# A macaron transformer block on one core: the second expert layer's scatters in eight pairs, each in a piece of its own

## The chip, the core and the metric

The kernel runs on one core of a Trainium2 chip. A core has five engines with queues of their own: PE (TensorE, matrix products), ACT (ScalarE, activation functions), DVE (VectorE, elementwise work and reductions), POOL (GpSimd, here mostly the issue of indirect DMAs) and SP (SyncE, plain DMAs). The time is the device time of one execution in microseconds (us); less is better.

## The reference

The input is one sequence of 4096 tokens with 256 features, in float32. Three residual steps follow each other:

```
x = x + 0.5 * ffn(layernorm(x))
x = x + attention(layernorm(x))        # 16 heads of 16
x = x + 0.5 * ffn(layernorm(x))        # the same weights as the first

ffn(x):  scores = softmax(x @ Wg)                  # 32 experts
         weights, indices = top_k(scores, 4)
         for e in 32 experts:
             tok = tokens that chose e              # at most 2048
             y[tok] += swiglu(x[tok], W1[e], W2[e], W3[e]) * w[tok]
         return y + swiglu(x, Ws1, Ws2, Ws3)        # a shared expert of width 256
swiglu = silu(x @ w1) * (x @ w3) @ w2
```

So each expert layer has to bring every token's row to four experts, and the attention lies between the two layers.

## The kernel before

The program has seven stages in order: `first_front` (normalizing, routing and the shared expert of layer 0), `Layer.experts` of layer 0, `projections` (queries, keys, values), `attention`, a tail inside `attention` (lines 1394 to 1440), `Layer.experts` of layer 1, and a last loop that adds up and stores.

**Routing** is `Layer.route` (lines 204 to 363), a Python generator. Every `yield` ends a *piece*: whoever drives the generator decides where in the program the next piece is placed. For a block of tokens it normalizes (L140 to L172), transposes on PE (L180), computes the gate (L233), takes the four largest scores (L254, L255), counts positions with two products (L276), works out slots (L293 to L342), and at its end sends rows: for each of its token tiles and each of the four choices POOL issues one indirect DMA (L353) which writes 128 rows of 264 floats to the slots named in `sidx`. In layer 0 a chunk has eight tiles (32 scatters), in layer 1 a block has four (16 scatters). The scatters declare no dependency on each other. `sidx`, an integer tile for the whole layer, is written by one DVE addition (L345); L346 and L347 then make the weights `wk`. All 16 scatters of a block lie in one piece.

**The attention loop** walks over 1024 steps: 8 blocks of 512 queries, 4 groups of 4 heads, 32 key tiles. In a step PE makes the scores of four heads two steps ahead (L1257), ACT takes exponentials (L1267) from PSUM banks in a ring, and PE multiplies them with the values (L1275). At a group's end DVE divides (L1295 to L1311). Hooks placed with `at(n, f)` run behind step n's value products: query loads (L1378), the addition of a shift to the queries (L1379), block loads (`load_x`, L1246 to L1248, called from L1381), the output projection of a finished block (`project_out`, L1353 and L1361), and the pieces of that block's way into layer 1. These last come from `front` (L1327): the pieces of `layer.route`, then for blocks 0, 1 and 2 those of `layer.shared` (the shared expert, L378 to L411), for blocks 3, 4 and 5 two stores; the shared expert of blocks 3 to 7 is done in the tail. `front` hands out `PIECES` = 24 calls, which are placed at every third step, in steps 3 to 24 of each group of the following block; there are 28 such places:

```
free = [
    m
    for m in range(n + 9, n + 1 + NG * NT)
    if 3 <= (m - n - 1) % NT <= 24 and (m - n - 1) % 3 == 0
]
for m, f in zip(free, front(b)):
    at(m, f)
```

A routed block needs ten pieces, so its scatters stand in the tenth, at step 45 of the following block. Blocks 0 to 6 are routed in the loop, block 7 in the tail.

**Order.** PE, ACT, DVE and SP keep the program's order (`manual_schedule` with ORDERED, L57); each engine works through its queue in order. A block's tokens lie in a tile `xq` of which there are two, so `load_x(nb)` can start once block nb - 2 is done with; it is called at step 2 of the last group of block nb - 1. Pieces that need a PSUM bank borrow the accumulator that is not in use (`Banks.tile`), and the steps beside them do with the ring alone.

**Tail.** After the last step, the shared expert of the blocks put off is interleaved with the route of block 7 by `next(route)`, and `share_out` prepares the extra blocks of the experts. `Layer.experts` then reads the scattered rows expert by expert.

Of the kernel before, what the change touches and what calls it, by code (L numbers as in the profile page):

```python
# [10 lines left out]
I32 = mybir.dt.int32  # L11
U32 = mybir.dt.uint32
AF = mybir.ActivationFunctionType
ALU = mybir.AluOpType
# [4 lines left out]
P = 128  # L19
# [14 lines left out]
QT = QB // P  # L34
# [6 lines left out]
K = 4  # L41
# [8 lines left out]
NSLOT = E * S0 + NOVMAX * BO  # L50
CLEARED = E * S0 + NOV * BO
LATER = (3, 4, 5, 6)
PIECES = 24
RW = D + 2 * K
KR = K + 1
BIG = float(1 << 20)
# [4 lines left out]
def kernel(  # L61
# [14 lines left out]
    nc = tc.nc  # L76
# [109 lines left out]
    class Layer:  # L186
# [17 lines left out]
        def route(self, ch, xt, pool, pm):  # L204
# [3 lines left out]
            n, t0 = self.n, ch * self.n  # L208
            count, held, total, shift = self.count, self.held, self.total, self.shift
            chunk = slice(t0, t0 + n)  # L210
            shape = [P, n, E]

            def tile(shape, name, dtype=F32, bufs=1):
                return pool.tile(shape, dtype, tag=name, name=name, bufs=bufs)
# [36 lines left out]
            top = tile([P, n, 8], "top")  # L251
# [87 lines left out]
            slot = tile([P, n, K], "slot")  # L339
# [2 lines left out]
                nc.vector.tensor_reduce(slot[:, :, k], hot[k][:], AX.X, ALU.add)  # L342
            beyond = tile([P, n, K], "beyond")
            nc.vector.tensor_scalar(beyond[:], slot[:], BIG, -BIG, ALU.is_ge, ALU.mult)
            nc.vector.tensor_add(self.sidx[:, chunk, :], slot[:], beyond[:])  # L345
            nc.vector.tensor_scalar(beyond[:], slot[:], BIG, 0.5, ALU.is_lt, ALU.mult)  # L346
            nc.vector.tensor_mul(self.wk[:, chunk, :], top[:, :, 0:K], beyond[:])  # L347


            group = f"scatter{self.index}"  # L350
            for t in range(n):
                for k in range(K):
                    ins = nc.gpsimd.indirect_dma_start(  # L353
                        out=self.xg[:],
                        out_offset=bass.IndirectOffsetOnAxis(
                            ap=self.sidx[:, t0 + t, k : k + 1], axis=0
                        ),
                        in_=xr[:, t, :],
                        in_offset=None,
                    ).ins  # L360
                    tc.declare_no_dep(ins, group=group, reason="rows of their own")
                    tc.add_to_no_dep_group(group, ins)
            yield

        def shared(self, ch, xt, xT, pool, pm):
# [801 lines left out]
    class Banks:  # L1167
# [18 lines left out]
        def tile(self, shape, dtype, tag, name):  # L1186

            self.lent = 1
            if self.over:
                self.next = (self.next + 1) % (self.RING + 2)  # L1190
            bank = self.all[:, self.next if self.over else self.other(), :]
            n = 1
            for m in shape[1:]:
                n *= m
            names = "abcd"[: len(shape) - 1]
            sizes = dict(zip(names, shape[1:]))
            return bank[:, :n].rearrange(f"p ({' '.join(names)}) -> p {' '.join(names)}", **sizes)
# [20 lines left out]
    def attention(layer, kT, v, shift, keep):  # L1218
# [5 lines left out]
        with (  # L1224
# [12 lines left out]
            def load_queries(b, g):  # L1237
                q = q_tiles[(b * NG + g) % 3]
                read_queries(q, b, g)
                qs[b, g] = q  # L1240

            def shift_queries(b, g):
                q = qs[b, g]
                nc.vector.tensor_scalar(q[:], q[:], shift[:], None, ALU.add)

            def load_x(b):  # L1246
                xs[b] = pool.tile([P, QT, D], F32, tag="x", name="xq")
                nc.sync.dma_start(xs[b][:], x1_at[:, b * QT : (b + 1) * QT, :])  # L1248
# [75 lines left out]
            def at(n, f):  # L1324
                later.setdefault(n, []).append(f)

            def front(b):  # L1327
# [18 lines left out]

                return [piece] * PIECES

# [26 lines left out]
            for n, (b, g, t) in enumerate(steps):  # L1375
                if t == 0 and n + NT < len(steps):
                    nb, ng, _ = steps[n + NT]
                    at(n + 2, lambda nb=nb, ng=ng: load_queries(nb, ng))  # L1378
                    at(n + 11, lambda nb=nb, ng=ng: shift_queries(nb, ng))  # L1379
                    if ng == 0:  # L1380
                        at(n + 2, lambda nb=nb: load_x(nb))  # L1381

            ahead = 2
# [15 lines left out]
            def half(b, xt, xT):  # L1399
                halves[b] = layer.shared_half(xt, xT, b * QT, pool, pm, bufs=2)  # L1400

            half(last - 1, xs[last - 1][:], layer.xT)
            for b in LATER[:-1]:
                both = pool.tile([P, HG, QB], F32, tag="ex", name="ex", bufs=3)
                n = NC * QB
# [6 lines left out]
            def go_on(b, pieces=1):  # L1412
                for _ in range(pieces):
                    next(halves[b])

            go_on(last - 1, 2)
            for i in range(0, QT, 2):
                project_out(last, i)
            route = layer.route(last, xs[last], pool, pm)
            next(route)  # L1420
            next(route)
            go_on(last - 1)
            go_on(LATER[0])
            for _ in range(NC + 1):
                next(route)
# [2 lines left out]
            for _ in range(3):  # L1428
                next(route)
            go_on(LATER[0])  # L1430
            for _ in range(2):
                next(route)
            half(last, xs[last][:], layer.xT)
            rest = [*LATER[1:-1], last]
            go_on(rest[0])
# [53 lines left out]
    with tc.tile_pool(name="keep0", bufs=1) as keep:  # L1489
        layer = Layer(0, keep, 2 * QT, nc.scalar.copy)  # L1490
        low = first_front(layer, keep)
        layer.experts(low)

        side = ctx.enter_context(tc.tile_pool(name="side", bufs=1, side="right"))
        with tc.tile_pool(name="kv", bufs=1, side="right", reuse_waits="tile") as kv:
            kT = kv.tile([P, NG, T], F32, name="kT")
            v = kv.tile([P, NT, NH, HV], F32, name="v")
            shift, flag = projections(layer, (side, kT, v))
            large = nc.values_load(flag[0:1, 0:1], min_val=0, max_val=1)
            with tc.If(large > 0):  # L1500
                take_maxima(kT)
            layer = Layer(1, side, QT, nc.vector.tensor_copy)
            attention(layer, kT, v, shift, side)
# [76 lines left out]
```

## Time and profile before

| what | value |
|---|---|
| median of 3 runs | 3525.7 us (3518.18 to 3526.12) |
| the profiled execution | 3541.41 us |
| its span, first to last instruction | 3539.7 us |
| PE busy | 3096.2 us (87%) |
| ACT busy | 2318.5 us (66%) |
| DVE busy | 954.2 us (27%) |
| POOL busy | 614.1 us (17%) |
| attention loop, first to last value product | 795 to 3091 us of the span |
| tail, then experts of layer 1 | from 3089 us and from some 3175 us |
| granted PE clock, mean | 0.934 |

The profile's page gives busy time by engine and by groups of instructions. A group's line names the source line, the engine, the operation and the tiles (out<-in), the count, then busy time and the mean of one in ns, then the engine's idle time ahead of it and what ended most of that. "issue" and "remote" stand for a wait whose releaser the profile does not show. The chain of work is the path followed back from the last instruction: start, length, what. A window row gives, for a stretch of time, the busy time and number of instructions of each engine, the granted PE clock as a share of full speed, and the DMA engines' share.

### The profile page before, as it was taken

Reading aid. Unit: us, or ns where it says so; the run is one execution under the profiler, and the core shown is the slowest. Engines: PE = TensorE matmul, PEld = TensorE weight load, DVE = VectorE, ACT = ScalarE, POOL = GpSimd, SP = SyncE. Lnnn points to the kernel's source line nnn. Section 1 sums busy time; section 2 is a strip of 40 time slices with the busy share of each in tenths; the row PEclk is TensorE's granted clock in tenths of the full one; section 3 lists DMA queues with packets and bytes.
Section 4 is the critical chain, followed back from the end, with each engine's and each line's share of the span. In section 5 each row is a group of like instructions: output and inputs, shape, how many; then the busy total and the mean of one; then the engine's idle time right before and its main releaser. Section 6 shows DMA issues by size and latency. Waiting matters only on the chain.

```text
span 3539.7 us, 50151 instructions
## 1 busy us (share of the span) xinstructions
PE 3096.2 (87%) x20043; PEld 1061.2 (30%) x20043; DVE 954.2 (27%) x2804; ACT 2318.5 (66%) x3732; POOL 614.1 (17%) x647
## 2 busy tenths in 40 slices
PE   5547886979999899899999989989989999979890
PEld 3224554432222222222222212212222221246550
DVE  5442334740002202211210210211121120154337
ACT  2101221449998799799889889989979988912220
POOL 3354654110000100100100010010010010025551
PEclk7678998989999999999999999999999999989995
DMA  6125665844110000000000000000000000036657
GB/s 239 69 87 191 223 216 175 238 128 141 57 38 3 25 16 3 27 16 3 23 19 3 16 33 3 15 33 4 9 33 10 3 18 10 21 121 226 222 194 302
DMA packets 141795, 284.07 MB, mean 80 GB/s; under 512 B 32480, under 2 KB 83296, under 8 KB 141152
## 3 DMA queue, kind: packets, MB, share of 16 engines
q1 hardware_dynamic: 90960, 176.85, 15.2%
q0 software_dynamic: 31872, 97.56, 7.7%
q10 hardware_dynamic: 18704, 6.20, 0.7%
q8 instruction: 163, 2.67, 0.3%
q14 instruction: 96, 0.79, 0.1%
HBM read 145.07 MB, written 131.27 MB: 78 GB/s over the span
## 4 chain that ended last, share of the span: by engine, by line
PE 71%; issue 3%; DVE 2%; DMA 1%; ACT 0%; another core or an unknown queue 0%; POOL 0%; SPq 0%; DVEq 0%; POOLq 0%; ACTq 0%
PE banks L1257 32%; PE banks L1275 29%; PE h L723 4%; PE o L745 2%; DVE xt L770 1%; PE xbt_ps L697 1%; PE banks L424 1%; PE banks L1353 1%; PE banks L378 1%; PE banks L446 0%; PE banks L233 0%; PE banks L398 0%; ACT ex L1267 0%; PE banks L180 0%
## 5 line engine op out<-in xcount | busy, mean ns | idle before, releaser
L1267 ACT ACTIVATE ex<-banks 128x512 f32<-128x512 f32 (+1 forms) x3224 | 2058.7, 714 | 230.8 <-PE banks L1257 110.6
L1257 PE MATMUL banks<-q,kT 32*128 32x512 f32 x8192 | 1188.6, 646 | 81.3 <-issue 42.8
L1275 PE MATMUL banks<-ex,v 128*17 128x512 f32 x8192 | 1085.5, 602 | 0.0
L353 POOL DMA_INDIRECT xg<-xr,sidx x256 | 246.5, 963 | 2413.5 <-DVE beyond L346 2226.9
L1257 PEld LDWEIGHTS banks<-q,kT 32*128 32x128 f32 x8192 | 330.8, 185 | 931.8 <-ACT ex L1267 746.6
L1295 DVE COPY o<-banks 128x512 f32<-128x512 f32 x32 | 22.1, 692 | 1403.4 <-ACT ex L1267 771.9
L1275 PEld LDWEIGHTS banks<-ex,v 128*17 128x17 f32 x8192 | 136.3, 95 | 785.2 <-issue 784.2
L753 POOL DMA_INDIRECT ys<-yb,toi x304 | 292.4, 962 | 218.9 <-DVE yb L751 83.3
L723 PE MATMUL h<-xT,w 128*128 128x512 f32 x512 | 251.3, 637 | 0.0
L732 ACT ACTIVATE s<-h 128x512 f32<-128x512 f32 (+1 forms) x112 | 51.7, 461 | 171.1 <-PE h L723 107.8
L703 ACT COPY xT<-xbt_ps 128x512 f32<-128x512 f32 (+1 forms) x112 | 50.6, 451 | 171.3 <-PE o L745 68.2
L745 PE MATMUL o<-w,hT 128*128 128x256 f32 x512 | 127.0, 389 | 18.9 <-issue 17.0
L723 PEld LDWEIGHTS h<-xT,w 128*128 128x128 f32 x512 | 101.5, 209 | 105.2 <-issue 105.2
L749 ACT COPY yb<-o 128x512 f32<-128x512 f32 x64 | 37.5, 586 | 118.6 <-PE o L745 81.1
L734 DVE TENSOR_TENSOR hT<-s,h 128x512 f32<-128x512 f32 (+1 forms) x112 | 57.8, 516 | 198.7 <-PE h L723 69.4
L1298 DVE RECIPROCAL den<-den 128x512 f32<-128x512 f32 x32 | 107.3, 3353 | 1.1
L745 PEld LDWEIGHTS o<-w,hT 128*128 128x128 f32 x512 | 93.6, 192 | 42.7 <-issue 29.0
L697 PE MATMUL xbt_ps<-ident,xb 128*128 128x128 f32 x512 | 74.1, 290 | 26.5 <-DMA xb<-xg 17.5
L770 DVE SCALAR_TENSOR_TENSOR xt<-y,wk,xt 128x256 f32<-128x256 f32 x192 | 93.1, 485 | 6.9
L701 DVE COPY xT<-xbt_ps 128x512 f32<-128x512 f32 (+1 forms) x112 | 57.9, 517 | 127.4 <-PE xbt_ps L697 86.9
L433 ACT ACTIVATE th<-sh_ps 128x512 f32<-128x512 f32 x16 | 9.2, 596 | 123.5 <-remote 70.5
L446 PE MATMUL so<-ws_sb,shT 128*128 128x256 f32 x128 | 47.4, 509 | 45.8 <-issue 23.7
(245 smaller groups left out, 1826.8 us busy)
## 6 DMA issues: line engine op xcount, KB each, us to landing
y<-ys SPq DMA_DIRECT2D x64, 640.0 KB
xb<-xg SPq DMA_DIRECT2D x62, 528.0 KB
w<-in_wexp_dram SPq DMA_DIRECT2D x64, 384.0 KB
xg<-zeros SPq DMA_DIRECT2D x152, 132.0 KB
xg<-zero SPq DMA_DIRECT2D x32, 264.0 KB
xbb<-xg SPq DMA_DIRECT2D x48, 132.0 KB
ys<-yb,toi POOLq DMA_INDIRECT x304
q<-qd SPq DMA_DIRECT2D x128, 34.0 KB
```

What stands on the lines that cost most here:

```text
L353: ins = nc.gpsimd.indirect_dma_start(out=self.xg[:], out_offset=bass.IndirectOffsetOnAxis(ap=self.sidx[:, t0 + t, k : k + 1], axis=0), in_ ...
L697: nc.tensor.transpose(tp[:, i * P : (i + 1) * P], xb[:, i, c * P : (c + 1) * P], ident[:])
L701: nc.vector.tensor_copy(xT[:, c, : n * P], tp[:, : n * P])
L723: nc.tensor.matmul(ps[:, : n * P], w[:, (j * NC + c) * H : (j * NC + c + 1) * H], xT[:, c, : n * P], start=(c == 0), stop=(c == NC - 1),)
L734: nc.vector.tensor_mul(hT[:, : n * P], s1[:, : n * P], h[1][:, : n * P])
L745: nc.tensor.matmul(o[:, i, :], hT[:, (i0 + i) * P : (i0 + i + 1) * P], w2, start=True, stop=True)
L753: ins = nc.gpsimd.indirect_dma_start(out=ys[:], out_offset=bass.IndirectOffsetOnAxis(ap=b["toi"][:, i : i + 1], axis=0), in_=yb[:, i, :], ...
L770: nc.vector.scalar_tensor_tensor(xt, y[:, k, :], self.wk[:, t, k : k + 1], y[:, K, :] if k == 0 else xt, ALU.mult, ALU.add,)
L1257: nc.tensor.matmul(pm.all[:, banks[j], :], kT[rows, g, t * P : (t + 1) * P], q[rows, :], start=True, stop=True,)
L1267: nc.scalar.activation(ex[:, i : i + n, :], pm.all[:, k : k + n, :], AF.Exp, scale=SCALE)
L1275: nc.tensor.matmul(acc[j * HP : j * HP + HV, :], v[:, t, g * HG + j, :], ex[:, j, :], start=(t == 0), stop=(t == NT - 1),)
L1298: nc.vector.reciprocal(den[:], den[:])
```

## The change

In layer 1 a block's 16 scatters are no longer in one piece: they go in eight pairs, and after each pair the generator yields, so each stands in a piece of its own, three steps behind the one before it. The final slots are left in the float tile `slot`, and ahead of each pair DVE copies the pair's two columns into a small integer tile `to` (16 of these), which the scatters of the pair use. In layer 0 the scatters stay together; there the addition that writes `sidx` moves behind the making of `wk`, in both layers `kept` is a tile of its own beside `beyond`. A routed block now has 18 pieces in place of ten, so `PIECES` grows to 28. `load_x(nb)` moves from the last group of block nb - 1 to step 2 of block nb itself. In the tail, the rest of the route is run to its end in place of two calls of `next`, so that the order there is as before apart from the copies.

```diff
-PIECES = 24
+PIECES = 28
...
             beyond = tile([P, n, K], "beyond")
             nc.vector.tensor_scalar(beyond[:], slot[:], BIG, -BIG, ALU.is_ge, ALU.mult)
-            nc.vector.tensor_add(self.sidx[:, chunk, :], slot[:], beyond[:])
-            nc.vector.tensor_scalar(beyond[:], slot[:], BIG, 0.5, ALU.is_lt, ALU.mult)
-            nc.vector.tensor_mul(self.wk[:, chunk, :], top[:, :, 0:K], beyond[:])
+            kept = tile([P, n, K], "kept")
+            nc.vector.tensor_scalar(kept[:], slot[:], BIG, 0.5, ALU.is_lt, ALU.mult)
+            nc.vector.tensor_mul(self.wk[:, chunk, :], top[:, :, 0:K], kept[:])
+            if self.index == 0:
+                nc.vector.tensor_add(self.sidx[:, chunk, :], slot[:], beyond[:])
+            else:
+                nc.vector.tensor_add(slot[:], slot[:], beyond[:])
...
             group = f"scatter{self.index}"
+
+            m = K if self.index == 0 else 2
             for t in range(n):
+                to = self.sidx[:, t0 + t, :]
                 for k in range(K):
+                    if self.index > 0 and k % m == 0:
+                        to = pool.tile([P, K], I32, tag="to", name="to", bufs=4 * QT)
+                        nc.vector.tensor_copy(to[:, k : k + m], slot[:, t, k : k + m])
                     ins = nc.gpsimd.indirect_dma_start(
                         out=self.xg[:],
-                        out_offset=bass.IndirectOffsetOnAxis(
-                            ap=self.sidx[:, t0 + t, k : k + 1], axis=0
-                        ),
+                        out_offset=bass.IndirectOffsetOnAxis(ap=to[:, k : k + 1], axis=0),
                         in_=xr[:, t, :],
                         in_offset=None,
                     ).ins
...
+                    if self.index > 0 and k % m == m - 1:
+                        yield
             yield
...
-                    if ng == 0:
+                    if ng == 1 and nb > 0:
                         at(n + 2, lambda nb=nb: load_x(nb))
...
-            for _ in range(2):
-                next(route)
+            for _ in route:
+                pass
             half(last, xs[last][:], layer.xT)
```

## The prediction

> **What bounds the kernel now.** I read the page's groups first, for who does the work and what the scatters cost their own engine.
>
> ```profile
> L1267 ACT ACTIVATE ex<-banks 128x512 f32<-128x512 f32 (+1 forms) x3224 | 2058.7, 714 | 230.8 <-PE banks L1257 110.6
> L1257 PE MATMUL banks<-q,kT 32*128 32x512 f32 x8192 | 1188.6, 646 | 81.3 <-issue 42.8
> ...
> L353 POOL DMA_INDIRECT xg<-xr,sidx x256 | 246.5, 963 | 2413.5 <-DVE beyond L346 2226.9
> ```
>
> The attention loop (795 to 3091 us) is two thirds of the span, and ACT and PE keep each other busy there: ACT's exponentials alone take 2058.7 of its 2296 us, and PE makes a step in 2.054 us. POOL is idle nearly throughout, so its 963 ns per scatter cost nothing as POOL time. The line to stop at is PE's 42.8 us of "issue": PE waits, and nothing visible lets it go.
>
> Then the chain of waits, in the stretch of the loop around one block's 16 scatters (POOL issues them from 2334.54 to 2354.4):
>
> ```profile
> 2340.16 0.98 PE banks L1275 x8
> 2341.14 1.29 issue
> 2342.43 1.14 PE banks L1257 x8
> 2343.57 0.98 PE banks L1275 x8
> 2344.56 8.51 issue
> 2353.06 2.09 PE banks L1257 x8
> 2355.15 2.20 PE banks L1275 x8
> ```
>
> Away from the burst the chain has 1.07 and 0.98 us for the two products of a step. Here PE loses 1.29 and 8.51 us, then runs at about half speed (2.09 and 2.20), and is back at 1.07 only from 2364.70 on. The same engine order, seen from ACT in the timeline:
>
> ```profile
> 2327.91 12.21 ACT L1267 ACTIVATE ex<-banks 128x512 f32<-128x512 f32 x18
> ...
> 2343.17 0.60 ACT L1267 ACTIVATE ex<-banks 128x512 f32<-128x512 f32 x1 [0.79 <-remote]
> ...
> 2352.41 0.60 ACT L1267 ACTIVATE ex<-banks 128x512 f32<-128x512 f32 x1 [6.75 <-remote]
> ```
>
> ACT's wait of 6.75 us ends first, PE's 8.51 us end at 2353.06, as soon as that exponential has freed its bank. All matmuls that ACT could be waiting for were over at 2344.6. So during a long run of scatters the engines stop getting work from each other. PE gaps of over 1 us inside the loop occur at the seven bursts and nowhere else.
>
> To price it I cut windows from one score product to another, each with exactly 13 steps, 104 instructions of L1257 (columns: window, length, PE busy, weight loads, granted clock, DMA share, GB/s). The first three are blocks with the shared expert, the next four without, the last is undisturbed.
>
> ```profile
> 1158.13:1204.45 46.32, 16.89 (x104) 4.67 (x104) 0.85 0.13 48
> 1454.87:1499.83 44.96, 15.18 (x104) 4.26 (x104) 0.89 0.14 49
> 1750.34:1795.69 45.35, 15.07 (x104) 4.26 (x104) 0.92 0.13 48
> 2046.12:2088.13 42.01, 16.50 (x104) 4.47 (x104) 0.88 0.14 52
> 2332.80:2374.85 42.05, 16.50 (x104) 4.47 (x104) 0.88 0.14 52
> 2619.52:2660.27 40.75, 15.99 (x104) 4.46 (x104) 0.87 0.15 54
> 2904.95:2947.90 42.95, 17.38 (x104) 4.67 (x104) 0.80 0.14 51
> 1000.00:1026.70 26.70, 14.82 (x104) 4.06 (x104) 1.00 0.15 53
> ```
>
> The seven sum to 304.39 us, seven undisturbed ones to 186.90: 117.5 us more. Each of the first three also holds three pieces of the shared expert, which the chain shows at 1.91 us apiece away from any burst (at 1190.47): 9 x 1.91 = 17.2. What is left, 100.3 us or 14.3 per burst, is the price of the bursts, clock loss included (0.80 to 0.92 in place of 1.00). DMA bandwidth isn't it: the undisturbed window has the same 53 GB/s, from clearing stores.
>
> **What the change does, part by part.**
>
> *The burst becomes eight pairs.* Pieces stand three steps apart, 3 x 2.054 = 6.2 us (more across a group's end). A pair takes POOL 2 x 0.96 + 0.30 = 2.2 us, so POOL rests about 4 us between pairs. What does a pair cost the loop? In the timeline ACT runs without a gap until 2340.12, 5.6 us after the first scatter, which is five scatters; in the burst of 1159.9 until 1167.5, 7.6 us. The experts' stage shows the recovery: its run of ten POOL issues from 3207.15 to 3219.5 has one PE gap of 1.16 us late in it, the run of twelve to 3237.2 ends in one of 2.89 us, the run of six from 3241.49 has none, with POOL pauses of only 2.3 to 4.3 us between. So the nearest row puts a pair at 0. The other bound is proportion, 100.3 / 112 = 0.9 us per scatter, under which pairs gain nothing. I take 0, because the first five scatters of a burst are the same operation in the same place. Gain: 100.3 us.
>
> *A rule against it.* The Trainium skill, "SBUF — State Buffer", section "Who interferes with whom", says that DMA never contends with a compute engine and that PE and ACT never wait on anyone. By the rule the bursts don't hold ACT, their spacing gains 0, and the sum would be 3528 us. The rows above show ACT and PE standing still in every long run of scatters. Measurement decides, and I use the row. It can't be an artefact of profiling either: the profiled execution took 3541.4 us, the median of the plain runs 3525.7, and those 15.7 us leave no room for 100.
>
> *Eight DVE copies per block.* The nearest row is the 128x1 COPY of L307, 0.147 us: 8 x 0.147 = 1.2 us. In the loop DVE is busy 5.93 of 100 us (window 2400 to 2500), so this hides; a query shift or a division queued behind a copy starts 0.15 us later, with steps to spare. In the tail it is not hidden: at 3138.76 PE has waited 9.54 us for DVE's u (L439), which stands behind the route, so all eight copies come ahead of it: +1.2 us (0 to 2). The tail's 16 scatters still follow each other, so its own stall stays.
>
> *POOL's new waits.* Each pair waits for its copy. Only the next pair is queued behind it on POOL, and its rows are read after the tail, some 200 us later at the closest: 0.
>
> *Layer 0.* The first scatter of each of four chunks now waits for two more DVE operations of 0.18 us (rows of L344 and L346): 0 to 1.6 us, I take 1.0 as three of the four bursts sit in a stretch where everything waits for them.
>
> *Pieces and borrowed banks.* The eight new pieces use no PSUM bank. The six shared pieces per block move eight places back and keep their 1.91 us each; 25 pieces fit the 28 places.
>
> *load_x.* It moves past 32 steps of SP's queue. Its buffer was given up by a store that stands ahead of it in that queue, and its first reader, the output projection, comes over 120 steps (250 us) later: 0. Were that cover gone, a 512 KB load at the page's best 302 GB/s would cost an estimated 1.7 us per block, 12 in all.
>
> Sum against the profiled execution: 3541.4 - 100.3 + 1.2 + 1.0 = 3443.3 us. Against the median, 15.7 lower: **3427.6, forecast 3428**.
>
> **Rivals.** *(B) A rest stays with each pair.* The smallest late release seen is ACT's 0.79 us above. 56 pairs x 0.79 = 44 us: 3472. For it: in these steps ACT has no slack. Against it: none of the first five scatters of any burst shows one. *(C) The stall goes by number.* If it came after so many scatters whatever their pace, two per block of half the length would give the same sum: about 3528. Against it: the experts' stage issues hundreds of indirect DMAs in runs of 6 to 18 and shows no wait of that size except late in a run. *(D) Slower.* Every pair makes ACT and PE miss one step, because a start of POOL from rest disturbs them (the first scatter of the burst at 1159.9 took 1.20 us in place of 0.96). Price 2.05 us, place the 56 pair pieces, 115 us against 100 saved: 3428 + 115 = 3543. It decides from 1.8 us per pair (100.3 / 56). Against it: burst starts show no missed step.
>
> **How the numbers follow.** A 0.76, B 0.13, C 0.03, D 0.08. A's own spread: the plain runs may stall 10% less than the profiled one (gain 90), the tail and layer 0 may cost 0 to 4; with the spread of the runs (8 us) that is 3415 to 3442. To leave out no more than two in ten the range goes up into B, to 3465. About 0.3% (10.6 us) is what a measurement of this kernel can tell from no change. Faster by more: A and B, 0.89; within: C, 0.03; slower: D, 0.08.
>
> **What would show it.** Right: windows of 13 steps around the pairs take 26.7 us plus 1.91 per shared piece, clock 1.00; "issue" on L1257 falls from 42.8 to a few us; ACT's "remote" waits vanish from the loop; 56 pairs of scatters some 6.2 us apart; the tail's PE wait on L439 is about 1 us longer. Wrong: gaps of ACT right behind each pair (B or D), or one long wait at about the fourth pair (C). The forecast falls if what holds ACT is not how long POOL issues without a rest.

## The result, and the profile after

The changed kernel takes 3481.2 us (median of 4 runs, 3479.16 to 3486.93); the kernel before took 3521.94 in the 4 runs beside it (3514.85 to 3526.12). The ratio is 0.9889 with an interval of 0.9866 to 0.9912. So it is faster, as forecast, but by 40.7 us (1.1%) where 98 were forecast, and 3481 lies outside the range of 3415 to 3465. The profiled execution took 3482.09 us, its span is 3480.4 us, its mean granted clock 0.941.

The page's groups, in the order in which those of before were shown (the change adds ten lines to this part of the program, so L1267 is now L1277, and L1257 is L1267):

```profile
L1277 ACT ACTIVATE ex<-banks 128x512 f32<-128x512 f32 (+1 forms) x3224 | 2058.0, 714 | 197.9 <-PE banks L1267 116.9
L1267 PE MATMUL banks<-q,kT 32*128 32x512 f32 x8192 | 1187.5, 646 | 63.5 <-ACT ex L1277 40.2
...
L363 POOL DMA_INDIRECT xg<-xr,to x128 | 123.8, 967 | 2223.8 <-DVE to L362 2189.3
```

PE's idle time ahead of the score products fell from 81.3 to 63.5 us only, and ACT's ahead of the exponentials from 230.8 to 197.9. The stalls are shorter, not gone. Why, is in POOL's timeline of the same block that the prediction looked at:

```profile
2303.42 0.96 POOL L363 DMA_INDIRECT xg<-xr,to  x1 [219.44 <-DVE to L362]
2304.68 0.96 POOL L363 DMA_INDIRECT xg<-xr,to  x1 [0.31 <-issue]
2305.95 0.96 POOL L363 DMA_INDIRECT xg<-xr,to  x1 [0.30 <-issue]
...
2312.29 0.96 POOL L363 DMA_INDIRECT xg<-xr,to  x1 [0.30 <-issue]
2355.50 1.01 POOL L363 DMA_INDIRECT xg<-xr,to  x1 [42.25 <-DVE to L362]
2356.82 0.96 POOL L363 DMA_INDIRECT xg<-xr,to  x1 [0.30 <-issue]
...
2364.42 0.96 POOL L363 DMA_INDIRECT xg<-xr,to  x1 [0.30 <-issue]
```

There are not eight pairs but two runs of eight scatters, 9.8 and 9.9 us long, with the same 0.30 us between scatters as before and one rest of 42.25 us. DVE's timeline, in the same window, says why:

```profile
2302.77 0.17 DVE L351 TENSOR_TENSOR slot<-slot,beyond 128x16 f32<-128x16 f32 x1
2302.97 0.38 DVE L362 CAST to<-slot 128x2 int32<-128x2 f32 x4
2348.01 0.69 DVE L1305 COPY o<-banks 128x512 f32<-128x512 f32 x1 [44.66 <-PE banks L1285]
...
2355.06 0.23 DVE L362 CAST to<-slot 128x2 int32<-128x2 f32 x2
2355.20 0.48 DVE L1254 TENSOR_SCALAR q<-q,shift 128x512 f32<-128x512 f32 x1
2355.60 0.23 DVE L362 CAST to<-slot 128x2 int32<-128x2 f32 x2
```

Four copies run in 0.38 us, one right behind the other, although three steps of PE's program stand between each and the next. Nothing in a copy waits for PE or ACT, and DVE does each as soon as it has done the one before. Only at the group's end does DVE's queue hold an instruction that waits for PE (44.66 us at L1305); the other four copies stand behind that. ACT's timeline shows what each run of eight then does:

```profile
2310.53 1.02 ACT L1277 ACTIVATE ex<-banks 128x1024 f32<-128x1024 f32 x1 [0.74 <-PE banks L1285]
2314.80 2.00 ACT L1277 ACTIVATE ex<-banks 128x512 f32<-128x512 f32 x3 [3.24 <-remote]
...
2363.33 2.77 ACT L1277 ACTIVATE ex<-banks 128x512 f32<-128x512 f32 x4 [1.80 <-PE banks L1285]
2367.00 5.86 ACT L1277 ACTIVATE ex<-banks 128x512 f32<-128x512 f32 x10 [0.90 <-PE banks L1285]
```

It is the shape of before on a smaller scale. Windows of 13 steps around the runs of eight (104 instructions of L1267; columns as before), here three around a block's first run, three around its second, and the sum over all 14:

```profile
1433.06:1465.22 32.16, 15.77 (x104) 4.27 (x104) 0.95 0.10 35
...
2301.38:2333.49 32.11, 15.78 (x104) 4.26 (x104) 0.95 0.10 34
2581.27:2613.42 32.15, 15.78 (x104) 4.27 (x104) 0.95 0.10 35
...
1483.92:1515.41 31.49, 15.59 (x104) 4.08 (x104) 0.95 0.10 35
...
2352.19:2382.02 29.83, 14.82 (x104) 4.06 (x104) 1.00 0.11 37
2632.13:2661.91 29.78, 14.83 (x104) 4.06 (x104) 1.00 0.10 37
...
sum 435.61, PE 216.31 PEld 58.71; mean PE 15.45 PEld 4.19
```

Undisturbed, 14 windows take 14 x 26.70 = 373.8 us, so the 14 runs of eight cost 61.8 us, 4.4 each. Before, seven runs of sixteen cost 100.3. The loop gives back 38.5 us, which is the 40.7 of the medians to within the spread of the runs. (The two profiled spans differ by 59.3 us. Of that, 38.8 lie in the loop, counted over all 1024 steps; the loop also starts 12.8 us earlier and the part behind it is 7.7 us shorter. The difference of the medians has no room for these two. For the 12.8 us a second execution of the changed kernel, shown below, makes spread likely: its first value product starts at 794.8 us of its span, against 782.5 in the first and 795.3 in that of before. The part behind the loop was as short there again, 440.2 us against 439.5, so that for the 7.7 us the cause stays open.)

One thing has to be known to read the numbers: the runs come in sets taken together on one chip, and in some sets no kernel stalls on scatters at all, the kernel before included, which then takes about 3256 us in place of 3522 or more; each experiment is therefore read against the kernel before of its own set, and only a set with stalls can tell the theories apart.

### The profile page after: what moved, and what is told of

Read it like the earlier page. It is cut to its first block, busy times and chain, and to the rows that moved or that the text cites. A ratio compares the mean times of both kernels' runs of the same rounds, so it can differ in the third digit from the quotient of the medians.

```text
span 3480.4 us, 50266 instructions
## 1 busy us (share of the span) xinstructions
PE 3077.2 (88%) x20043; PEld 1056.3 (30%) x20043; DVE 955.5 (27%) x2868; ACT 2317.8 (67%) x3732; POOL 616.2 (18%) x647
## 4 chain that ended last, share of the span: by engine, by line
PE 70%; DVE 3%; issue 2%; POOL 1%; DMA 1%; another core or an unknown queue 1%; ACT 1%; SPq 0%; DVEq 0%; POOLq 0%; ACTq 0%
PE banks L1267 32%; PE banks L1285 29%; PE h L733 3%; DVE xt L780 1%; PE o L755 1%; POOL ys L763 1%; PE xbt_ps L707 1%; PE banks L1363 1%; PE banks L388 1%; ACT ex L1277 1%; PE banks L434 0%; PE banks L233 0%; PE banks L456 0%; DMA ys<-yb,toi 0%
## 5 line engine op out<-in xcount | busy, mean ns | idle before, releaser
L1277 ACT ACTIVATE ex<-banks 128x512 f32<-128x512 f32 (+1 forms) x3224 | 2058.0, 714 | 197.9 <-PE banks L1267 116.9
L1267 PE MATMUL banks<-q,kT 32*128 32x512 f32 x8192 | 1187.5, 646 | 63.5 <-ACT ex L1277 40.2
L1267 PEld LDWEIGHTS banks<-q,kT 32*128 32x128 f32 x8192 | 329.7, 184 | 912.2 <-ACT ex L1277 770.3
L363 POOL DMA_INDIRECT xg<-xr,to x128 | 123.8, 967 | 2223.8 <-DVE to L362 2189.3
L1305 DVE COPY o<-banks 128x512 f32<-128x512 f32 x32 | 22.1, 691 | 1317.2 <-PE banks L1285 712.5
L733 PE MATMUL h<-xT,w 128*128 128x512 f32 x512 | 241.3, 616 | 0.0
L363 POOL DMA_INDIRECT xg<-xr,sidx x128 | 123.7, 966 | 149.7 <-issue 104.3
```

Source lines behind the costliest of these rows:

```text
L363: ins = nc.gpsimd.indirect_dma_start(out=self.xg[:], out_offset=bass.IndirectOffsetOnAxis(ap=to[:, k : k + 1], axis=0), in_=xr[:, t, :], i ...
L733: nc.tensor.matmul(ps[:, : n * P], w[:, (j * NC + c) * H : (j * NC + c + 1) * H], xT[:, c, : n * P], start=(c == 0), stop=(c == NC - 1),)
L1267: nc.tensor.matmul(pm.all[:, banks[j], :], kT[rows, g, t * P : (t + 1) * P], q[rows, :], start=True, stop=True,)
L1277: nc.scalar.activation(ex[:, i : i + n, :], pm.all[:, k : k + n, :], AF.Exp, scale=SCALE)
```

## The experiments

**Theory 1**: pairs cost nothing, but the copies don't keep them apart; make each copy wait for the loop, and the forecast gain comes. **Rival 1**: the pairs are apart well enough, and what is left goes with every pair or every scatter (B and C of the prediction). **Rival 2**: the rest of the gain was lost elsewhere, to `load_x` or the tail.

### Paced pairs

Each copy also reads two elements of the exponentials that ACT made last, times zero. The slots stay the same; the copy can't run before that step. In the tail, where there is no loop, the copy is plain.

```diff
...
-                        nc.vector.tensor_copy(to[:, k : k + m], slot[:, t, k : k + m])
+                        if self.gate is None:
+                            nc.vector.tensor_copy(to[:, k : k + m], slot[:, t, k : k + m])
+                        else:
+                            nc.vector.scalar_tensor_tensor(
+                                to[:, k : k + m],
+                                self.gate[:, 0, 0:m],
+                                0.0,
+                                slot[:, t, k : k + m],
+                                ALU.mult,
+                                ALU.add,
+                            )
...
+                layer.gate = ex
...
```

> The changed kernel with one edit: the operation that makes a pair's integer slots also reads the exponentials of the step that its piece stands behind (times zero), so that DVE cannot make it before ACT has got there. In the trace of the changed kernel nothing held the copies back: four of them ran within 0.4 us, and the scatters went in two runs of eight per block. Theory 1 (what holds ACT and PE is how long POOL issues without a rest; the pieces alone space nothing): pairs now stand some 6.2 us apart, the excess of the loop over its step time falls from 160 us to some 99 us, and the time is 3481 - 61 = about 3420. Theory 2 (the stall goes by the number of scatters, whatever their pace): still two stalls per block, about 3480. Theory 3 (each pair leaves a rest of some 0.8 us): 56 x 0.8 = 45, about 3465.

Measured 3256.32 us (13 runs) against 3255.88 for before, ratio 1.0003 (0.9995 to 1.0011): a set without stalls, so nothing was there to win. Three other sets were of the same kind: 3257.14 against 3255.6, 3254.58 against 3254.5, 3256.33 against 3258.22, no interval further from 1 than 0.0012. Their expectations, which differ little:

> The paced pairs of the first experiment once more. There the kernel before took 3256 us and had no stalls, so nothing could be told apart; between the two sets the same kernel took 3534 us with stalls. If the kernel before takes some 3525 us here: theory 1 (only an unbroken run of POOL DMA issues holds the others, the first five to eight are free) 3525 - 100 = about 3425, with the loop's excess back at some 99 us; theory 2 (it goes by number) about 3485; theory 3 (each pair leaves 0.8 us) about 3470. If it takes 3256, all three are the same as before.

> The paced pairs a third time; of the sets so far the second alone ran with stalls (the kernel before took 3534 us there, 3256 in the two others). If the kernel before takes some 3525 us here: theory 1 (only an unbroken run of POOL's DMA issues holds the others, the first five to eight are free) about 3425, with the loop's excess at some 99 us; theory 2 (by number of scatters) about 3485; theory 3 (each pair leaves 0.8 us) about 3470. If it takes 3256, the paced pairs take 3256.

> The paced pairs once more. If the kernel before takes some 3525 us here (stalls present): theory 1 (only an unbroken run of POOL's DMA issues holds the others, the first five to eight are free) about 3425, with the loop's excess over its step time at some 99 us; theory 2 (by number of scatters, whatever the pace) about 3485, excess 158; theory 3 (each pair leaves 0.8 us) about 3470. If the kernel before takes 3256, the paced pairs do too.

Then a set with stalls. 

> The paced pairs once more, for a set with stalls. If the kernel before takes some 3525 us here: about 3425 if only an unbroken run of POOL's DMA issues holds the others; about 3485 if it goes by number; about 3470 if each pair leaves 0.8 us. If the kernel before takes 3256, the paced pairs do too.

Measured 3420.25 us (3419.04 to 3421.46) against 3521.8 (3517.75 to 3530.18): ratio 0.9708, interval 0.9665 to 0.9750, 101.6 us faster (two executions against three). Of its profile, DVE's and POOL's timeline around the first pairs of a block (the copy is L366, the scatter L374):

```profile
2274.09 0.16 DVE L366 SCALAR_TENSOR_TENSOR to<-ex,slot 128x2 int32<-128x2 f32 x1 [4.07 <-ACT ex L1288]
2280.26 0.16 DVE L366 SCALAR_TENSOR_TENSOR to<-ex,slot 128x2 int32<-128x2 f32 x1 [6.00 <-ACT ex L1288]
```

```profile
2274.53 0.96 POOL L374 DMA_INDIRECT xg<-xr,to  x1 [2.01 <-DVE to L366]
2275.79 0.96 POOL L374 DMA_INDIRECT xg<-xr,to  x1 [0.30 <-issue]
2280.69 0.96 POOL L374 DMA_INDIRECT xg<-xr,to  x1 [3.94 <-DVE to L366]
2281.96 0.96 POOL L374 DMA_INDIRECT xg<-xr,to  x1 [0.31 <-issue]
```

Now DVE waits for ACT at the copies (a block's very first one is due at once), and from the second pair on the pairs are 6.2 us apart and POOL rests 3.94 us between them, the 4 us of the prediction. The score products' group (L1278 here) and windows of 13 steps around four pairs each, with the sum over 14 such windows:

```profile
L1278 PE MATMUL banks<-q,kT 32*128 32x512 f32 x8192 | 1178.1, 641 | 18.5 <-DVE q L1265 17.6 <-ACT ex L1288 0.9
```

```profile
2268.19:2294.89 26.70, 14.82 (x104) 4.06 (x104) 1.00 0.11 41
...
sum 373.84, PE 207.55 PEld 56.87; mean PE 14.83 PEld 4.06
```

373.84 us against 14 x 26.70 = 373.8: 56 pairs cost 0.0 us, the clock is 1.00, and PE's wait for exponentials is down to 0.9 us. That the stalls were there in this execution too shows ahead of the loop: its first value product starts at 786.5 us, in the first of the sets without stalls, with the same kernel, at 661.7. From its first to its last value product the loop takes 2195.5 us here and 2195.6 there, so pacing gives back all that scatters cost the loop. Theory 1 stands, rival 1 falls, and so does rival 2: this kernel has the moved load and the changed tail, and has the whole gain.

### The changed kernel again

The same kernel, to see whether the two runs of eight and their price repeat. 

> The changed kernel as it is, beside the kernel before. In the first three experiments the kernel before took 3256 us in place of 3522, with its bursts of 16 unaltered, and no wait of ACT for an unseen releaser was left in the loop. Theory 1 (the stall belongs to the chip or its condition at the time, and the bursts are only where it shows): where it is absent the changed kernel is the same as before, 3256 within 0.1%, and where it is present some 1% faster. Theory 2 (the changed kernel has a gain of its own beside the stalls, for instance the 20 us of the first comparison that do not lie in the loop): 3236 where the stall is absent.

Measured 3495.64 us (3492.4 to 3500.36) against 3533.98, ratio 0.9895 (0.9877 to 0.9914). Again two runs of eight per block (2309.81 to 2319.64 and 2362.01 to 2371.89 in the same block). From the score products of the first step to those of the last the loop takes 158.3 us more than 1023 x 2.054; the first execution took 160.3, before 199.05, paced pairs 97.5 with stalls and 97.6 without (query shifts, shared pieces and the like, which all have).

### Only the later loads

Before, with nothing but `load_x` moved.

```diff
-                    if ng == 0:
+                    if ng == 1 and nb > 0:
                         at(n + 2, lambda nb=nb: load_x(nb))
```

> The kernel before with only the block load moved to step 2 of its own block; scatters as before in one burst of 16. If the load has no part in the gain, as the sum had it: within 0.3% of before, about 3522. If part of the 41 us comes from it, it would be up to 20 us faster (3502).

Measured 3256.59 us (20 runs) against 3255.88, ratio 1.0003 (0.9996 to 1.0010). The move costs nothing in this set. The profile is worth more for what it shows of a set without stalls: a block's 16 scatters in one unbroken run,

```profile
2141.95 0.96 POOL L353 DMA_INDIRECT xg<-xr,sidx  x1 [251.45 <-DVE beyond L346]
2143.21 0.96 POOL L353 DMA_INDIRECT xg<-xr,sidx  x1 [0.30 <-issue]
...
2160.92 0.96 POOL L353 DMA_INDIRECT xg<-xr,sidx  x1 [0.30 <-issue]
```

and ACT beside it without a gap, and the window of 13 steps around it:

```profile
2137.81 37.56 ACT L1267 ACTIVATE ex<-banks 128x512 f32<-128x512 f32 x55
```

```profile
2140.25:2166.96 26.71, 14.83 (x104) 4.06 (x104) 1.00 0.23 82
```

The scatters, their order and their durations are those of the bursts that cost 14.3 us each elsewhere. Whether a burst stalls the loop is thus not decided by the kernel alone. One more thing tells the two kinds of set apart. The profile's list of DMA issues has the time from issue to landing behind the count; first before, then this kernel:

```profile
xg<-xr,sidx POOLq DMA_INDIRECT x256
```

```profile
xg<-xr,sidx POOLq DMA_INDIRECT x256, 2.4
```

In none of the six profiles with stalls could POOL's indirect DMAs be matched with a landing; in all fourteen without, those of the scatters to `xg` land 2.4 to 2.5 us after their issue (median). It is a lead to the cause and no more: the traces don't tell whether the landings were late, or only their records lost.

### A burst of 64

Before, with 48 more scatters of the same rows into three spare buffers behind a block's 16; the work added is only these.

```diff
...
+            if self.index > 0:
+                for r in range(3):
+                    for t in range(n):
+                        for k in range(K):
+                            ins = nc.gpsimd.indirect_dma_start(
+                                out=spare[r][:],
...
```

> The kernel before, and behind each of a block's 16 scatters of layer 1 another 48 that send the same rows into three spare buffers, so that POOL issues for some 80 us without a rest, eight times. If the run length at which engines begin to be held has only moved (from 6 to 10 us in the first traces to over 20 us here), ACT must show waits late in these bursts, up to 7 x 60 us in the loop: 3256 + 100 to 420. If POOL's issuing holds nobody under this condition, the loop keeps its time; the tail's burst of 64 then delays the last expert layer by 48 x 1.26 = 61 us at most, 3256 to 3320.

Measured 4044.5 us against 3533.98, ratio 1.1445 (1.1418 to 1.1471). Three views of it: ACT's longest group of waits in the loop (us in total, times, longest), its timeline during one burst (POOL issues from 2588.22 on, for 64 x 1.26 = 81 us), and the window of 13 steps around that:

```profile
ACT ex L1282 <- remote: 378.1, 48, 27.5
```

```profile
2598.28 1.02 ACT L1282 ACTIVATE ex<-banks 128x1024 f32<-128x1024 f32 x1 [0.85 <-PE banks L1290]
2605.35 0.60 ACT L1282 ACTIVATE ex<-banks 128x512 f32<-128x512 f32 x1 [6.05 <-remote]
...
2634.85 0.60 ACT L1282 ACTIVATE ex<-banks 128x512 f32<-128x512 f32 x1 [22.11 <-issue]
2640.45 0.60 ACT L1282 ACTIVATE ex<-banks 128x512 f32<-128x512 f32 x1 [5.00 <-PE banks L1290]
2651.65 1.02 ACT L1282 ACTIVATE ex<-banks 128x1024 f32<-128x1024 f32 x1 [10.60 <-remote]
2675.45 0.60 ACT L1282 ACTIVATE ex<-banks 128x512 f32<-128x512 f32 x1 [22.78 <-remote]
```

```profile
2586.53:2690.59 104.06, 17.70 (x104) 4.70 (x104) 0.64 0.23 83
```

104.06 - 26.70 = 77.4 us lost to a run of 81; by the starts of the steps all seven bursts in the loop lose 75 to 79. With the other sizes this makes a row: a run of 2.2 us costs 0, of 9.8 costs 4.4 on average (a block's first run 1.8 to 6.3 and mostly 5.4, its second 3.1 to 4.8), of 20 costs 14.3, of 81 costs 77.4. A run costs about its length less some 5 us. The loss goes with the unbroken run, not with the number of scatters in a block: 16 of them cost 14.3 us in one run and 0 in paced pairs. As each scatter takes 1.26 us in every run, its time and its count can't be told apart.

### Fours, and what in a run holds the loop

Paced, with four scatters behind each copy (`m = 4`) in place of two. 

> As the paced pairs, but four scatters to a piece (four pieces per block). A four takes POOL 5.06 us of the 6.16 us between pieces, so it rests 1.1 us. In the bursts seen so far ACT's first gap came 5.4 to 7.6 us after the first scatter, so a four by itself is at the edge. Theory 1 with a short rest being enough: about 3420 to 3430. Theory 1 with a rest of 1.1 us too short to clear what has piled up: stalls return in the second and third four of a block, 3445 to 3480. Theory 2: about 3480.

Measured 3255.81 us against 3255.88, ratio 1.0001 (0.9992 to 1.0009): no stalls in the set, so inconclusive.

Bytes or issuing: paced pairs, and 16 more scatters per block that carry rows of 32 bytes (`xr[:, t, 0:8]`) into a spare buffer. 

> The paced pairs, and behind a block's last pair one burst of 16 further indirect DMAs that send only the first 8 floats of each row (32 bytes in place of 1056) into a spare buffer. POOL's time and the number of descriptors are those of the old burst, the bytes a 33rd. In a condition with stalls: if the bytes hold the engines, the time is that of the paced pairs; if POOL's issuing or the descriptors do, each of seven bursts costs 14 us again, 100 us more than the paced pairs.

3249.13 us against 3255.6, one run, no stalls; two other sets were the same (3257.91 against 3254.5; 3255.74 against 3258.22, 0.9993, 0.9984 to 1.0002). Then a set with stalls. 

> The paced pairs (3420 us in a set with stalls) with one further burst per block of 16 indirect DMAs of 32 bytes per row. With stalls: 3420 if the bytes hold the engines, 3420 + 7 x 14.3 = 3520 if POOL's issuing or the number of descriptors does. Without stalls: 3256.

Measured 3484.58 us against 3539.3, ratio 0.9848 (0.9819 to 0.9876). It is not the burst that I meant: the extra scatters don't depend on each other and came among the pairs, two behind each from the first pair on. POOL's timeline shows per block one run of eight, half of it short rows, and six runs of four:

```profile
2309.10 0.96 POOL L376 DMA_INDIRECT xg<-xr,to  x1 [0.31 <-issue]
2310.36 0.96 POOL L389 DMA_INDIRECT spare<-xr,to  x1 [0.30 <-issue]
2311.63 0.96 POOL L389 DMA_INDIRECT spare<-xr,to  x1 [0.30 <-issue]
...
2316.68 0.96 POOL L389 DMA_INDIRECT spare<-xr,to  x1 [0.30 <-issue]
2322.54 0.95 POOL L376 DMA_INDIRECT xg<-xr,to  x1 [4.90 <-DVE to L368]
```

In this block the steps beside the run of eight lost 5.8 us, those beside the six fours 1.4 us together. Step by step against the loop of the paced pairs, the seven runs of eight lost 2.9 to 5.8 us, 4.8 on average, where eights of full rows cost 4.4. So some half of the bytes made a run of eight no cheaper: what weighs is the issue of the DMAs, or the number of rows sent, which stayed, and not the bytes. The 42 runs of four, 4.7 us long, with rests of mostly 1 to 5 us between them, cost 0.4 us each. Both fit a loss of about the run's length less 5 us, both read from an arrangement that wasn't planned.

POOL busy, or POOL issuing DMAs: paced pairs, and 64 additions of 128x128 on POOL (0.46 us each, no DMA) behind a block's last pair. 

> The paced pairs, and behind a block's last pair 64 additions of 128x128 on POOL over a scratch tile, some 16 to 25 us of POOL work without any DMA. In a condition with stalls: if POOL being busy is enough to hold ACT and PE, some 100 us more than the paced pairs; if it takes the issue of DMAs, the same as the paced pairs, within 0.3%.

> Paced pairs, and behind each block's last pair 64 POOL additions of 128x128 (0.46 us each, 29 us without a rest, no DMA among them). In a set in which the kernel before stands at about 3522 us: if the loss comes from POOL issuing DMAs without a rest, the additions are free and this is 3420 us like the paced pairs. If any 29 us of unbroken POOL work held the loop, seven blocks would each lose about 25 us: some 3595 us. In a set in which the kernel before stands at about 3256 us both give 3256 and nothing is told apart.

3255.74 against 3255.6, 3258.48 against 3254.5, and 3256.75 against 3256.14 (18 runs, 0.9998, 0.9990 to 1.0005). Three sets without stalls. Sixteen plain DMAs issued by POOL instead: 

> The paced pairs, and behind a block's last pair 16 plain DMAs on POOL's queue, each storing the 128 rows of one tile to a spare buffer: the bytes and the count of the old burst, without indices. In a condition with stalls: if the indirect form is what holds the engines, the same as the paced pairs; if any run of DMAs issued by POOL does, up to 100 us more, less if a plain issue takes POOL less than 1 us.

3259.34 us against 3255.6, likewise. A last kernel carried the additions in the even blocks and, in the odd ones, an unbroken run of 16 scatters of 32-byte rows that waits for one vector of slots:

```diff
...
+            if self.gate is not None and ch % 2 == 0:
...
+                for _ in range(64):
+                    nc.gpsimd.tensor_tensor(gated, gated, zeros[:, 0:P], ALU.add)
+            elif self.gate is not None:
...
+                for i in range(n * K):
+                    ins = nc.gpsimd.indirect_dma_start(
+                        out=spare[:],
+                        out_offset=bass.IndirectOffsetOnAxis(ap=again[:, i : i + 1], axis=0),
+                        in_=xr[:, i // K, 0:8],
...
```

> Paced pairs, and behind the last pair of blocks 0, 2, 4 and 6 the 64 POOL additions (29 us, no DMA), behind that of blocks 1, 3 and 5 sixteen extra scatters of 32-byte rows in one unbroken run (20 us; they wait for one vector of slots, so that nothing else comes among them). Read block by block, in a set in which the kernel before stands at about 3522 us. If it takes DMA issues without a rest, whatever their bytes: the even blocks lose nothing and each odd one about 14 us, 3420 + 43 = 3463 us. If it takes bytes on their way: nothing anywhere, 3420. If any unbroken POOL work suffices: also some 24 us in each even block, 3560. In a set in which the kernel before stands at 3256 us, all give 3256.

3256.27 us against 3258.39, ratio 0.9997 (0.9987 to 1.0007): no stalls. Whether POOL has to issue DMAs, or only to be busy, to hold the loop stays open.

## Why the prediction was wrong, point by point

**What bounds the loop, and the price of the bursts: right.** The prediction took 100.3 us for the seven bursts and 0 for a pair. Paced pairs gave 101.6 us against the kernel before of their set, and their 14 windows come to 0.0 us above the undisturbed. The forecast of 3428 describes that kernel (3420.25), not the one that was changed.

**The step that failed**: "Pieces stand three steps apart, 3 x 2.054 = 6.2 us (more across a group's end). A pair takes POOL 2 x 0.96 + 0.30 = 2.2 us, so POOL rests about 4 us between pairs." A piece's place in the program is three steps behind the one before, but that is a place in DVE's queue, and DVE is not held to the steps: with 5.93 us of work in 100 it goes through its queue until something in it needs PE. The prediction used that very number to say that the copies hide, and didn't see that it also lets them run together. What was there in place of eight pairs is two runs of eight, because four copies stand ahead of the group's end and four behind; their price, 61.8 us instead of 0, accounts for the miss (forecast gain 98, less 61.8, is 36; measured 40.7, with 8 us between executions of one kernel). That something was gained at all was luck: the tenth place happens to be the fourth from last in its group, so that the division at the group's end cut one run of sixteen into two of eight. The copies stood next to each other in DVE's order, with no instruction between them that waits for the loop. That could be read before the run.

**"Each pair waits for its copy"** was true (DVE to L362 ends 2189.3 us of POOL's idle time), and of no use, as the copy itself waited for nothing.

**The rivals.** B gave 3472, nearest in number, by a rest of 0.79 us with each pair; paced pairs have no such rest. C, a stall by number whatever the pace, falls with the paced pairs, whose 16 scatters per block stall nothing. D, a missed step per pair, falls with the windows of 26.70. None named what happened: the change not doing what it says. The experts' stage, from which the prediction took that runs of six are free and that ten and twelve end in gaps of 1.16 and 2.89 us, gave the right order but too small a price for the loop, where eights cost 4.4.

**The rule against it.** The Trainium skill, "SBUF — State Buffer", section "Who interferes with whom", says that DMA doesn't contend with compute engines and that PE and ACT wait on no one. Taken that widely, the runs contradict it in sets with stalls (77.4 us lost beside one run of 64 scatters) and agree in the others (26.71 us beside a run of 16). But the section speaks of the ports of SBUF, and no run shows that the stall arises there: it may be right about the ports and still not promise what the prediction read in it.

**"It can't be an artefact of profiling"** was right on thin grounds. The prediction compared a profiled execution with plain ones by their times; but two executions of one kernel can also differ by 266 us for a reason outside the kernel, as the sets show, so 15.7 us between two times says little about a cause. The better ground came later: the medians of after and of paced pairs lie 40.7 and 101.6 us under those of before, as the traces say.

**Copies, tail, layer 0, load_x.** The tail's PE wait for u is 10.0 us, 0.5 longer (forecast 1.2). `load_x` cost nothing in the set where it was moved alone. Layer 0's 1.0 us can't be told from the spread; in sets without stalls paced pairs, which have all these edits, are within 0.1% of before (1.0003, 0.9995 to 1.0011), so together they are worth less than 4 us.

**Its size elsewhere.** Between the profile of before and that of a set without stalls, 286.4 us are lost: 100.6 in the loop, 137.6 ahead of it, 48.1 behind it. The scatters of layer 0 and the indirect DMAs of the experts stand there, also in long runs. That pacing those would win is argued, not tried.

## What to carry to other kernels

A place in the program ordered DVE's copies here and paced nothing: DVE ran through its queue until an instruction in it waited for PE. To space an engine's work by another's progress, give it an operand that the other makes at that point, and look in the order of the engine in between for whatever it can run ahead to. And before a gain is priced per piece, ask which instruction makes the piece wait.

The fastest version here is paced pairs: 0.9708 of before where scatters stall the loop, 1.0003 where they don't. Against the changed kernel it is some 60 us less where there are stalls; the two were not run in one set, each was measured against before in its own.

## What the runs showed of the hardware

In the sets with stalls, an unbroken run of indirect DMAs on POOL holds ACT and PE after about its first 5 us, for about the rest of its length: 4.4 us of 9.8, 14.3 of 20, 77.4 of 81. In pairs of 2.2 us with rests of 3.94 us it is free. ACT's waits then end at "remote" or "issue", in single pieces up to 27.5 us, and the granted PE clock falls with the gaps (0.64 in the window of the 64).

Whether it does so changes from set to set, with the same kernel: before takes 3255 us with bursts of 16 that cost nothing, or 3522 and more. Four sets had stalls and six had none, and one and the same chip number showed both at different times. What turns it on, and through which resource POOL holds the others, no run here settles; that the landings of POOL's DMAs can be matched in one kind of set only is the one lead.
